# A two-layer kernel on one core: the skip connection moved from layer 1 into the row dispatch, and layer 1's operations placed anew

## The chip, the core and the metric

The kernel runs on one core of a Trainium2 chip. The core has five instruction streams: TensorE (PE, matrix products into PSUM), VectorE (DVE), ScalarE (ACT), GpSimd (POOL) and SyncE (SP, which here only issues DMAs). Each stream runs its instructions in the order of its own queue and waits on semaphores for the others. The metric is the device time of one execution in microseconds (us), lower is better.

## The reference

The input x is 32 images of 128 channels and 56x56 pixels, fp32. Two layers follow one another.

Layer 0 is a depthwise 7x7 convolution, a LayerNorm over channels, and a mixture of experts on the T = 100352 normalized rows of 128 channels: each row is routed to its two best of 8 experts, an expert takes 15680 rows at most in order of priority, and each row's result comes back scaled by its gate.

```
logits = xf @ Wg + bg
topv, topi = jax.lax.top_k(logits, K)            # K = 2
...
h = gelu(einsum('ecd,edf->ecf', eb, W1) + b1)
y = einsum('ecf,efd->ecd', h, W2) + b2
...
return input + x_skip + moe_out
```

So layer 0's output is a sum of three things: the image itself, the normalized rows, and what the experts add.

Layer 1 is a 1x1 convolution (cv1), a branch with a 3x3 depthwise convolution, and a branch with a Mamba block: LayerNorm, a projection to 256 channels and a gate z, a causal convolution over 4 positions, and a state space recurrence with 16 states per channel over the 3136 positions of an image:

```
def step(h, inp):
    dA_t, dBu_t, C_t = inp
    h = dA_t * h + dBu_t
    return (h, jnp.einsum('bds,bs->bd', h, C_t))
```

dA is exp(dt * A), dBu is dt * B * x. The two branches are joined by a second 1x1 convolution and added to the layer's input.

## The kernel before

**Layer 0.** The convolution runs first (to about 1500 us) and writes the normalized rows into `res_d` in DRAM. Within each image row of 56 pixels the rows lie in reversed order. Then the routing is worked out (to 1766 us): for each row two slots in `buf_d`, and two gates.

*Dispatch* (1773 to 3939 us) takes 14 columns of 112 rows at a time, 56 times. SP loads them from `res_d` into `xg0`; ScalarE copies them to `xg1` (line 854, 128x1792 values); VectorE writes a gate and a row number, taken from the table `backs`, behind each row in both (lines 856, 857); and GpSimd issues 14 indirect DMAs from each of the two, each of which scatters 128 rows of 130 words into `buf_d` (line 859), 1568 in all. The tiles `xg` have 6 buffers, so loads run ahead. A scatter waits for the completion of the one eight before it. Half way through, `weights` prepares layer 1's constants on several engines. This part of the kernel is ordered by an automatic scheduler.

*Experts* (3940 to 5881 us) load tiles of 128 rows from `buf_d`, transpose them, run the two matrix products with Gelu between, scale by the gate, and add the result into `res_d` at the rows' places by 984 indirect scatter-adds that GpSimd issues (line 911).

**Layer 1** (5883 us to the end) takes an image in NQ1 = 7 groups of CH1 = 448 positions, 224 groups in all, and in each group 16 *units*, one per state. The 256 channels lie as 128 partitions x 2 halves. What is done once in a group:
- `fetch` loads x1 (the image's 448 positions) and yg (four tiles of 112 rows of `res_d`).
- `moe_pe` puts both into one PSUM tile: x1 by a product with the identity (line 1026), and each tile of yg by a product with `perm`, a permutation that turns the rows back into their order (line 1028). `moe_act` copies the sum to x1.
- cv1, the LayerNorm's factor (`rstd_act`, three small VectorE steps `rstd_dve`, of which steps 0 and 1 work in `aside`, a corner of the PSUM buffer da0), the projections, and dt (`sp_...`); `du_pool` is dt times the input on GpSimd (line 1245).
- `dd_pe` begins the PSUM sum py; `yz_dve` multiplies the finished sum by the gate; `out_pe` and `out_act` end the group.

What is done for each unit:
- `bc_load`: SP loads B and C, broadcast over partitions, for a pair of units.
- `db_pool`: GpSimd's product of du and B for a pair of units (line 1336, 128x1792).
- `exp_act`: ScalarE's two exps, one per half, into the PSUM buffer `da[u % 2]` (line 1354), so units take turns in two buffers.
- `scan_dve`: VectorE's recurrence over both halves (line 1373), in place in da, or into a tile `hs`.
- `cmul`: the product with C, on VectorE from da or on GpSimd from hs (line 1397).
- `carry_act`: ScalarE copies the last state to the head of db for the next group.
- `sum_pe`: TensorE adds the product into py (line 1286).

`MODE` has a letter for each unit: D has scan and product on VectorE; P has the scan into hs and the product on GpSimd; Q is P with the scan in two halves; M (not used before) splits the unit, first half with the product on VectorE, second half on GpSimd.

The order is written out by hand. `PLAN` and `UNITS` give each operation a key, a due time in units; all operations of all groups are sorted by 16 times the group (plus the unit) plus the key, and issued in that order, which so becomes the order of every engine's queue.

Of the kernel before, what the change touches and what calls it, by code (L numbers as in the profile page):

```python
# [13 lines left out]
C = 128  # L14
RW = C + 2
HW = 56
# [26 lines left out]
MODE = 'DQDDQDPPDDDDPDDP'  # L43
PRODS = 6
PLAN = (
    (-41.157, "fetch"),
    (-34.382, "moe_pe"),
    (-32.986, "moe_act"),
    (-28.346, "cv1_pe", "p_cvc", "cv1c"),
    (-27.384, "sq_act"),  # L50
    (-26.393, "cv1_pe", "p_cv1", "cv1t"),
    (-25.274, "cv1_act"),
    (-23.306, "var_pe"),
    (-23.291, "rstd_act"),
    (-23.185, "edges_act"),
    (-20.935, "rstd_dve", 0),
    (-20.876, "rstd_dve", 1),
    (-19.458, "rstd_dve", 2),
    (-19.126, "bc_pe"),
    (-18.367, "te_dve"),  # L60
    (-18.165, "te_act"),
    (-17.77, "z_pe", 0),
    (-16.927, "z_copy", 0),
    (-15.982, "z_pe", 1),
    (-15.86, "xm_pe", 0),
    (-15.811, "xm_pe", 1),
    (-14.784, "z_copy", 1),
    (-14.441, "z_silu"),
    (-14.388, "xm_act", 0),
    (-14.349, "xm_act", 1),  # L70
    (-13.504, "tables"),
    (-13.487, "px_pe"),
    (-11.507, "px_act"),
    (-11.215, "dt_pe", 0),
    (-10.684, "dt_pe", 1),
    (-10.326, "sp_abs", 0),
    (-9.043, "sp_abs", 1),
    (-8.458, "sp_exp"),
    (-7.656, "sp_one"),
    (-6.228, "sp_w"),  # L80
    (-5.252, "sp_pe", ("w", "e", "m")),
    (-5.135, "sp_ln"),
    (-5.019, "sp_pe", ("u",)),
    (-4.678, "lt_pe", range(0, 9)),
    (-4.117, "sp_act", 0),
    (-3.918, "sp_act", 1),
    (-3.032, "lt_act", 0),
    (-3.001, "du_pool"),
    (-2.343, "lt_act", 1),
    (2.033, "lt_silu"),  # L90
    (3.656, "dd_pe"),
    (18.599, "yz_dve", 0),
    (18.857, "yz_dve", 1),
    (23.328, "out_pe"),
    (25.003, "out_act"),
# [3 lines left out]
        (-5.892, "bc_load", "bb"),  # L99
        (-3.501, "bc_load", "cb"),  # L100
        (-2.818, "db_pool"),
        (-0.991, "exp_act"),
        (-0.076, "scan_dve"),
        (0.16, "cmul", 0),
        (1.245, "carry_act"),
        (3.662, "sum_pe"),
    ),
    (
        (-2.505, "db_pool"),
        (-0.83, "exp_act"),  # L110
        (-0.619, "scan_dve"),
        (1.229, "cmul", 0),
        (3.088, "carry_act"),
        (9.441, "sum_pe"),
    ),
    (
        (-11.504, "bc_load", "bb"),
        (-2.533, "bc_load", "cb"),
        (-2.288, "db_pool"),
        (-0.633, "exp_act"),  # L120
        (-0.074, "scan_dve"),
        (0.16, "cmul", 0),
        (1.407, "carry_act"),
        (3.828, "sum_pe"),
    ),
    (
        (-3.007, "db_pool"),
        (-1.559, "exp_act"),
        (-0.609, "scan_dve"),
        (-0.338, "carry_act"),  # L130
        (0.16, "cmul", 0),
        (2.009, "sum_pe"),
    ),
    (
        (-4.093, "bc_load", "bb"),
        (-3.639, "db_pool"),
        (-0.666, "bc_load", "cb"),
        (-0.482, "exp_act"),
        (0.865, "scan_dve"),
        (1.06, "cmul", 0),  # L140
        (1.786, "sum_pe"),
        (2.033, "carry_act"),
    ),
    (
        (-4.025, "db_pool"),
        (-1.052, "exp_act"),
        (-0.068, "scan_dve"),
        (0.16, "cmul", 0),
        (1.263, "carry_act"),
        (3.791, "sum_pe"),  # L150
    ),
    (
        (-5.791, "bc_load", "bb"),
        (-4.743, "db_pool"),
        (-2.416, "bc_load", "cb"),
        (-0.463, "exp_act"),
        (0.538, "scan_dve"),
        (0.678, "cmul", 0),
        (1.758, "carry_act"),
        (4.239, "sum_pe"),  # L160
    ),
    (
        (-5.64, "db_pool"),
        (-0.299, "exp_act"),
        (-0.211, "scan_dve"),
        (1.06, "cmul", 0),
        (5.047, "sum_pe"),
        (5.187, "carry_act"),
    ),
    (  # L170
        (-7.178, "bc_load", "bb"),
        (-4.153, "db_pool"),
        (-3.514, "bc_load", "cb"),
        (-1.218, "exp_act"),
        (-0.956, "scan_dve"),
        (0.16, "cmul", 0),
        (0.466, "carry_act"),
        (0.815, "sum_pe"),
    ),
    (  # L180
        (-4.714, "db_pool"),
        (-1.825, "exp_act"),
        (-0.406, "scan_dve"),
        (0.16, "cmul", 0),
        (0.742, "carry_act"),
        (1.653, "sum_pe"),
    ),
    (
        (-8.23, "bc_load", "bb"),
        (-5.573, "bc_load", "cb"),  # L190
        (-4.053, "db_pool"),
        (-1.1, "exp_act"),
        (-0.6, "scan_dve"),
        (0.16, "cmul", 0),
        (0.996, "carry_act"),
        (1.077, "sum_pe"),
    ),
    (
        (-3.777, "db_pool"),
        (-0.685, "exp_act"),  # L200
        (-0.409, "scan_dve"),
        (0.16, "cmul", 0),
        (1.104, "sum_pe"),
        (1.278, "carry_act"),
    ),
# [39 lines left out]
def tile_kernel(tc: tile.TileContext, a: dict, out: bass.AP):  # L245
# [14 lines left out]
    with (  # L260
# [573 lines left out]
        with (  # L834
# [13 lines left out]
            for q in range(QB):  # L848
# [15 lines left out]
                if q == QB // 2:  # L864
                    w3 = weights(w3p, w3t, p3t)
# [600 lines left out]
```

## Time and profile before

| What | Value |
|---|---|
| Median of 14 runs | 15851.67 us (15842.47 to 15862.2) |
| Profiled execution | 15851.65 us, span 15849.9 us from first to last instruction |
| Dispatch, from first scatter to last | 1773.05 to 3939.4 us |
| Experts | 3940 to 5881 us |
| Layer 1 | 5883 to 15849.9 us |
| Scatters of dispatch | 1568, busy 1647.1 us |
| ScalarE copies of xg | 56, mean 1.688 us |
| db products of layer 1 | 1792 (8 a group), mean 3.685 us |
| Whole scans of layer 1 | 2240 in da, 896 in hs, mean 2.02 and 2.01 us |

How to read the profile's lines. A line of a group has the source line, the engine, the operation, output <- inputs with partitions x elements, the count; then the busy time in us and the mean of one in ns; then the idle time of the engine just ahead of these instructions and what ended it. "issue" is time in which the engine waited for nothing that the profile shows. A line of the timeline has the start, the duration, the instruction, and in brackets the idle time before. In the slices, the span is cut into 40 equal parts, and each digit is an engine's busy share in tenths. In the table by stretch, each row has the bounds and the length of the stretch and each engine's busy time with its count of instructions; PEclk is TensorE's granted clock as a share of its full speed. Neighbouring instructions of VectorE and GpSimd overlap a little in the records, so a row of back-to-back instructions is measured from start to start.

### The profile page before, as it was taken

The numbers are of one execution on the slowest core, as the hardware profiler recorded it, in microseconds if no ns is written. First come the engines' busy times: TensorE is split into PE (matmuls) and PEld (weight loads), VectorE is DVE, ScalarE is ACT, GpSimd is POOL, SyncE is SP. The second block draws the span as 40 slices with busy tenths as digits, with TensorE's granted clock in tenths as the row PEclk, the third lists the DMA queues.
The fourth block names the chain that finished last, engine by engine and source line by source line (L and its number), as shares of the span: only waits on it lengthen the run. The fifth ranks groups of instructions, "written<-read, shape, count | busy, mean of one in ns | idle before, by whom it ended". The sixth has DMA issues, their size and how long they took to land. (4 is left out here: it accounts for less than half of the span.)

```text
span 15849.9 us, 247520 instructions
## 1 busy us (share of the span) xinstructions
PE 12824.6 (81%) x92981; PEld 7167.3 (45%) x92981; DVE 11116.6 (70%) x11366; ACT 10499.5 (66%) x21038; POOL 13337.8 (84%) x6330
## 2 busy tenths in 40 slices
PE   7996200000999999999999999999999999999998
PEld 7996100000777764444444444444444444444444
DVE  2655400000111119999999999999999999999999
ACT  4564200000444448888888888888888888888888
POOL 2443477777888879999999999999999999999999
PEclk9997555555999999999999999999999999999999
DMA  8885422222555545555555555555555555555555
GB/s 262 233 239 175 170 72 71 71 71 64 69 71 71 71 65 184 184 184 185 185 184 184 184 185 184 182 185 184 183 183 185 184 184 185 184 184 184 184 183 171
DMA packets 1325280, 2520.85 MB, mean 159 GB/s; under 512 B 139352, under 2 KB 777136, under 8 KB 1316400
## 3 DMA queue, kind: packets, MB, share of 16 engines
q1 hardware_dynamic: 1127600, 2310.57, 46.8%
q0 software_dynamic: 196480, 194.45, 7.2%
q8 instruction: 732, 11.99, 0.3%
q14 instruction: 468, 3.83, 0.1%
HBM read 2129.06 MB, written 375.43 MB: 158 GB/s over the span
## 5 line engine op out<-in xcount | busy, mean ns | idle before, releaser
L1336 POOL TENSOR_TENSOR db<-du,bb 128x1792 f32<-128x1792 f32 x1792 | 6582.7, 3685 | 1.2 <-DMA bb<-bc_d 1.0
L1354 ACT ACTIVATE da<-dt,aneg 128x449 f32<-128x449 f32 x7168 | 4540.0, 637 | 374.7 <-DVE r L1095 112.9
L1373 DVE TENSOR_TENSOR_SCAN da<-da,db 128x898 f32<-128x898 f32 x2240 | 4522.3, 2019 | 0.6 <-issue 0.5
L1286 PE MATMUL py<-prod,ident 64*64 64x448 f32 x28672 | 3224.9, 547 | 124.2 <-DVE prod L1397 115.7
L1397 POOL TENSOR_TENSOR prod<-hs,cb 128x896 f32<-128x896 f32 x1344 | 2606.9, 1940 | 239.1 <-issue 151.9
L1397 DVE TENSOR_TENSOR prod<-da,cb 128x896 f32<-128x896 f32 x2240 | 2438.6, 1089 | 136.2 <-DMA cb<-bc_d 18.9
L859 POOL DMA_INDIRECT buf_d<-xg,slot x1568 | 1647.1, 1050 | 523.2 <-issue 519.0
L911 POOL DMA_INDIRECT res_d<-ys,xb x984 | 1592.0, 1618 | 349.9 <-issue 282.6
L951 PE MATMUL ept<-ident,xb 128*128 128x128 f32 (+1 forms) x984 | 189.0, 274 | 2078.1 <-DMA xb<-buf_d 2077.7
L1373 DVE TENSOR_TENSOR_SCAN hs<-da,db 128x898 f32<-128x898 f32 x896 | 1784.7, 2012 | 0.1
L1286 PEld LDWEIGHTS py<-prod,ident 64*64 64x64 f32 x28672 | 1008.7, 132 | 1561.9 <-issue 1045.7
L1126 PE MATMUL p_xm<-te,wk 128*128 128x448 f32 x3584 | 1395.5, 540 | 0.0
L903 DVE TENSOR_TENSOR ys<-py,b2t 128x512 f32<-128x512 f32 (+2 forms) x256 | 170.8, 670 | 1729.2 <-PE py L897 1466.9
L856 DVE COPY xg<-gate 128x14 f32<-128x14 f32 x112 | 20.4, 185 | 1884.3 <-DMA buf_d<-xg,slot 1846.8
L854 ACT COPY xg<-xg 128x1792 f32<-128x1792 f32 x56 | 94.5, 1688 | 1821.4 <-DMA buf_d<-xg,slot 1775.8
L951 PEld LDWEIGHTS ept<-ident,xb 128*128 128x128 f32 (+1 forms) x984 | 124.6, 143 | 2081.8 <-issue 2080.8
L897 PEld LDWEIGHTS py<-w2t,hh 128*128 128x128 f32 x7872 | 937.9, 191 | 191.6 <-issue 118.9
L897 PE MATMUL py<-w2t,hh 128*128 128x128 f32 x7872 | 987.4, 278 | 14.8 <-ACT hh L893 9.4
L1126 PEld LDWEIGHTS p_xm<-te,wk 128*128 128x128 f32 x3584 | 671.8, 189 | 665.7 <-issue 568.0
L379 PE MATMUL pc<-xc,toep 112*112 112x112 f32 (+1 forms) x8192 | 938.2, 270 | 40.1 <-ACT toep L368 36.3
L1258 PE MATMUL p_l<-xh,dwd 64*64 64x224 f32 x16128 | 907.3, 352 | 21.9 <-ACT dt L1240 1.8
L1377 DVE TENSOR_TENSOR_SCAN hs<-da,db 128x449 f32<-128x449 f32 x896 | 924.5, 1073 | 0.5 <-ACT da L1354 0.3
(241 smaller groups left out, 20283.2 us busy)
## 6 DMA issues: line engine op xcount, KB each, us to landing
bb<-bc_d SPq DMA_DIRECT2D x1792, 448.0 KB
cb<-bc_d SPq DMA_DIRECT2D x1792, 448.0 KB
toep<-toep_d SPq DMA_DIRECT2D x448, 392.0 KB
buf_d<-zero SPq DMA_DIRECT2D x28, 2275.0 KB
xb<-buf_d SPq DMA_DIRECT2D x240, 260.0 KB
xt<-in_x SPq DMA_DIRECT2D x32, 1568.0 KB
res_d<-xa SPq DMA_DIRECT2D x128, 392.0 KB
xg<-res_d SPq DMA_DIRECT2D x56, 896.0 KB
```

Source lines behind the costliest of these rows:

```text
L379: nc.tensor.matmul(pc[:, c, :, lo:hi], lhsT=tp[c // 2][:, c % 2, 6 - 2 * o : 8 - 2 * o, :], rhs=s4[:, c, :, lo + o - 1 : hi + o - 1], star ...
L859: apart(nc.gpsimd.indirect_dma_start(out=buf_d[:, :], out_offset=bass.IndirectOffsetOnAxis(ap=slots[k][:, o + j : o + j + 1], axis=0), in_ ...
L897: nc.tensor.matmul(py[:n, j, :], lhsT=hh[:, k, j * 128 : j * 128 + n], rhs=w2t[:, k, :], start=k == 0, stop=k == KF - 1,)
L911: apart(nc.gpsimd.indirect_dma_start(out=res_d[:, :], out_offset=bass.IndirectOffsetOnAxis(ap=xb[:n, j, C + 1 : C + 2].bitcast(I32), axis= ...
L1126: nc.tensor.matmul(p[:, :CH1], lhsT=s["wk"][:, k, hs], rhs=d["te"][:, k : k + CH1], start=k == 0, stop=k == DC - 1 and not first,)
L1258: nc.tensor.matmul(d["p_l"][r][k * HD : (k + 1) * HD, : CH1 // 2], lhsT=s["dwd"][rs, t, rs], rhs=d["xh"][rs, dy + k * R : dy + (k + 1) * R ...
L1286: nc.tensor.matmul(ps[r][h * HD : (h + 1) * HD, :CH1], lhsT=lhsT(rs, h), rhs=rhs[rs, h, :], start=start, stop=stop,)
L1336: nc.gpsimd.tensor_tensor(dbp[i // 2].rearrange("p k (h t) -> p k h t", h=2)[:, :, :, 1:], st[g]["du"].unsqueeze(1).to_broadcast(both), un ...
L1354: e = nc.scalar.activation(da[:, h * W1 : (h + 1) * W1], st[g]["dt"][:, h, :], AF.Exp, scale=s["aneg"][:, h, i : i + 1])
L1373: scans.append(nc.vector.tensor_tensor_scan(hs, da, dbs[i], 0.0, ALU.mult, ALU.add))
L1377: scans.append(nc.vector.tensor_tensor_scan(hs2[h][:, hh], da[:, hh], dbs[i][:, hh], 0.0, ALU.mult, ALU.add))
L1397: eng.tensor_tensor(w["prod"], w["hs"][0][:, :, 1:], w["cb"], ALU.mult)
```

## The change

The change has two parts.

**In layer 0's dispatch** a new function `skip` makes the sum of image and normalized rows for half an image at a time, 64 parts, and stores it into a new DRAM tensor `sum_d` in the rows' natural order. The experts now add into `sum_d`, so their row numbers `backs` are made in that order, too. Layer 1 reads only `sum_d`, and `moe_pe` only transposes. The copies of xg move from ScalarE to VectorE; `perm` is made in the dispatch rather than at the program's start; ScalarE copies the skip's sums out of PSUM and issues their stores.

```
-        mean_w = const.tile([128, 128], F32, name="mean_w")
+        mean_w = const.tile([128, 1], F32, name="mean_w")
...
-            nc.tensor.matmul(p[:, 0:1], lhsT=mean_w, rhs=cv1b, start=True, stop=True)
+            mean_c = wt.tile([128, C], F32, name="mean_c")
+            nc.vector.memset(mean_c, 1.0 / C)
+            nc.tensor.matmul(p[:, 0:1], lhsT=mean_c, rhs=cv1b, start=True, stop=True)
...
+            def skip(n, h):
+                t0 = (n * TPI + h * HT) * TT
+                xt = sk.tile([C, HT * TT], F32, name="xs")
+                nc.sync.dma_start(out=xt, in_=x_d[n, :, h * HT * TT : (h + 1) * HT * TT])
+                xr = sk.tile([TT, HT, C], F32, name="xr")
+                rows = [v[t0 : t0 + HT * TT, :].rearrange("(k p) c -> p k c", p=TT) for v in (res_d, sum_d)]
+                nc.sync.dma_start(out=xr, in_=rows[0])
+                for j0 in range(0, HT, 4):
+                    w = min(4, HT - j0)
+                    p = psk.tile([TT, 4, C], F32, name="p_sk")
+                    nc.tensor.matmul(p[:, :w], lhsT=perm, rhs=xr[:, j0 : j0 + w], start=True, stop=False)
+                    for j in range(w):
+                        nc.tensor.matmul(
+                            p[:, j, :], lhsT=xt[:, (j0 + j) * TT : (j0 + j + 1) * TT], rhs=ident,
+                            start=False, stop=j == w - 1,
+                        )
+                    nc.scalar.copy(xr[:, j0 : j0 + w], p[:, :w])
+                nc.scalar.dma_start(out=rows[1], in_=xr)
...
-                    nc.scalar.copy(xgs[1][:, :, :C], xgs[0][:, :, :C])
+                    nc.vector.tensor_copy(xgs[1][:, :, :C], xgs[0][:, :, :C])
...
+                    for _ in range(-(-len(parts) // (TT // XT * (QB - q) - p0 // XT))):
+                        skip(*parts.pop(0))
...
-                        out=res_d[:, :],
+                        out=sum_d[:, :],
```

HT is 14, so a part is 14 tiles of 112 rows. The tiles of `skip` have 2 buffers, its PSUM tiles 3.

**In layer 1** the modes and all keys are new, exp is issued by halves with a key each, hs has 3 buffers and x1 has 4 instead of 5. The lists of which operations touch different bytes (`near`, `free`, `decay`, where `halves` and `apart` stood) are kept in another way.

```
-MODE = 'DQDDQDPPDDDDPDDP'
+MODE = 'PPDDMDPPDDPDPDDD'
...
-    (-41.157, "fetch"),
-    (-34.382, "moe_pe"),
+    (-60.5589, "fetch"),
+    (-32.6293, "moe_pe"),
...
-    (-20.935, "rstd_dve", 0),
-    (-20.876, "rstd_dve", 1),
-    (-19.458, "rstd_dve", 2),
+    (-22.4112, "rstd_dve", 0),
+    (-22.4112, "rstd_dve", 1),
+    (-20.1575, "rstd_dve", 2),
...
-    (-4.117, "sp_act", 0),
-    (-3.918, "sp_act", 1),
-    (-3.001, "du_pool"),
+    (-3.7463, "sp_act", 0),
+    (-3.7368, "sp_act", 1),
+    (-1.8387, "du_pool"),
...
 UNITS, unit 4:
-        (-4.093, "bc_load", "bb"),
-        (-3.639, "db_pool"),
-        (-0.666, "bc_load", "cb"),
-        (-0.482, "exp_act"),
-        (0.865, "scan_dve"),
-        (1.06, "cmul", 0),
-        (1.786, "sum_pe"),
-        (2.033, "carry_act"),
+        (-7.6159, "bc_load", "bb"),
+        (-3.5327, "db_pool"),
+        (-3.253, "bc_load", "cb"),
+        (-0.0755, "exp_act", 0),
+        (0.2559, "exp_act", 1),
+        (0.491, "scan_dve", 0),
+        (0.705, "scan_dve", 1),
+        (0.9114, "cmul", 0),
+        (1.0371, "cmul", 1),
+        (1.0707, "carry_act"),
+        (3.718, "sum_pe"),
...
-            d["x1"] = three.tile([C, CH1], F32, name="x1", bufs=5)
-            nc.sync.dma_start(out=d["x1"], in_=x_d[n, :, q * CH1 : (q + 1) * CH1])
...
-            nc.tensor.matmul(p[:, :CH1], lhsT=ident, rhs=d["x1"], start=True, stop=False)
             for j in range(TPC1):
-                nc.tensor.matmul(
-                    p[:, j * TT : (j + 1) * TT], lhsT=yg[:, j, :], rhs=perm, start=False, stop=j == TPC1 - 1
-                )
+                nc.tensor.transpose(p[:, j * TT : (j + 1) * TT], yg[:, j, :], ident[:TT, :TT])
```

The order in which VectorE goes through a group is new with the keys. From unit 0 on it has: scans 0, 1, 2, 3, product 2, the two yz, product 3, the half scans of 4, half product 4, scan 5, product 5, scans 6, 7, 8, product 8, scan 9, rstd steps 0 and 1, product 9, scans 10, 11, rstd step 2, product 11, scans 12, 13, 14, product 13, te, product 14, scan 15, product 15. GpSimd makes the whole products of units 0, 1, 6, 7, 10 and 12 and half of unit 4.

## The prediction

> **What bounds the kernel now.** I read the page first, then the busy time by stage, then the groups of the steady part of layer 1, then the order of single instructions on VectorE and GpSimd, and last the row scatters of the dispatch. The page, engines and slices:
>
> ```profile
> PE 12824.6 (81%) x92981; PEld 7167.3 (45%) x92981; DVE 11116.6 (70%) x11366; ACT 10499.5 (66%) x21038; POOL 13337.8 (84%) x6330
> DVE  2655400000111119999999999999999999999999
> POOL 2443477777888879999999999999999999999999
> ```
>
> No engine leads by much, and the shares mix stages. From the sixteenth slice on (5883 us, layer 1) VectorE and GpSimd are full; in slices 5 to 9 (dispatch) VectorE is nearly idle and GpSimd issues scatters. The busy time by stage, one stretch inside the dispatch and one inside layer 1:
>
> ```profile
> core 0: us, PE busy (x) PEld busy (x) DVE busy (x) ACT busy (x) POOL busy (x), PEclk, DMA share, GB/s
> 2450.00:4600.00 2150.00, 641.18 (x3632) 462.19 (x3633) 133.54 (x306) 332.43 (x450) 1659.61 (x1388) 0.65 0.32 69
> 7000.00:15500.00 8500.00, 8137.87 (x60065) 3817.92 (x60064) 8375.80 (x6537) 7392.12 (x15322) 8166.82 (x2940) 1.00 0.58 184
> ```
>
> In layer 1 VectorE is busy 98.5%, GpSimd 96.1%, TensorE 95.7%: VectorE bounds it, the two others stand close behind. The groups of that stretch:
>
> ```profile
> L1336 POOL TENSOR_TENSOR db<-du,bb 128x1792 f32<-128x1792 f32 x1538 | 5649.5, 3685 | 1.0 <-DMA bb<-bc_d 1.0
> L1397 POOL TENSOR_TENSOR prod<-hs,cb 128x896 f32<-128x896 f32 x1154 | 2238.3, 1940 | 198.9 <-issue 125.2 <-DMA cb<-bc_d 29.4 <-DVE r L1095 27.8
> L1397 DVE TENSOR_TENSOR prod<-da,cb 128x896 f32<-128x896 f32 x1922 | 2092.4, 1089 | 117.4 <-DMA cb<-bc_d 18.3 <-PE p_var L1073 1.6 <-issue 1.3
> L1245 POOL TENSOR_TENSOR du<-dt,xm 128x896 f32<-128x896 f32 x192 | 371.7, 1936 | 133.3 <-ACT dt L1240 129.9 <-DMA cb<-bc_d 2.9
> L1354 ACT ACTIVATE da<-dt,aneg 128x449 f32<-128x449 f32 x6150 | 3895.1, 637 | 315.6 <-DVE r L1095 97.8 <-DVE prod L1397 80.1 <-DVE hs L1377 4.8
> L1028 PE MATMUL p_moe<-perm,yg 112*128 112x112 f32 x1536 | 200.2, 273 | 0.0
> L1026 PE MATMUL p_moe<-x,ident 128*128 128x448 f32 x384 | 195.6, 591 | 0.0
> ```
>
> 1538 db products at 8 per group are 192.25 groups: 8500/192.25 = 44.2 us per group, 224 groups in all. GpSimd is busy 8166.82/192.25 = 42.5 us of each and waits 0.69 for dt and 1.03 ahead of products; TensorE is busy 42.3. On VectorE the distance from start to start matters, because neighbours overlap:
>
> ```profile
> 10017.17 3.93 DVE L1373 TENSOR_TENSOR_SCAN hs<-da,db 128x898 f32<-128x898 f32 x2
> 10021.03 2.01 DVE L1373 TENSOR_TENSOR_SCAN da<-da,db 128x898 f32<-128x898 f32 x1
> 10023.13 1.09 DVE L1397 TENSOR_TENSOR prod<-da,cb 128x896 f32<-128x896 f32 x1
> 10024.13 2.03 DVE L1373 TENSOR_TENSOR_SCAN da<-da,db 128x898 f32<-128x898 f32 x1
> ```
>
> A scan followed by another scan takes 1.93 (two in 3.86), a product 1.00 to 1.01, and a scan followed by its own product 2.10 to 2.13: about 0.12 to 0.17 is spent on the result that the next instruction reads.
>
> **Layer 1, VectorE.** Before, per group: 14 whole scans x 1.94, 2 pairs of half scans x 1.98, 10 products x 1.01, 7 of them directly behind their scan (+0.12), and 2.03 of yz, te and rstd: 27.16 + 3.96 + 10.10 + 0.84 + 2.03 = 44.09, against 44.2 measured. After: 15 whole scans, one pair (unit 4, mode M), 9 products and a half (0.52), and by the new order only 3 directly behind their scan: 29.10 + 1.98 + 9.09 + 0.52 + 0.36 + 2.03 = 43.08. So 1.01 us less work per group.
>
> **Layer 1, GpSimd.** It keeps 8 db, 6 whole products and du, and gains half a product: 0.97 (half of 1.94) to 1.07 (with some fixed part). 42.5 + 1.0 = 43.5 becomes its floor. The wait for dt goes (du_pool is queued some 5 us behind sp_act), and most of the product waits with it. GpSimd is thus slower than VectorE's bare 43.08: the group cannot fall below 43.5.
>
> **Layer 1, waits that the new order adds.** A scan needs both exps of its unit, 0.64 us each, and an exp can only overwrite its da buffer when the scan and VectorE product of two units before, or rstd's use of da0, are done. In the new order rstd steps 0 and 1 stand ahead of product 9 and then scan 10: exp 10 starts when rstd 1 has left da0, only product 9 (1.01) covers its two halves (1.28 plus a hand-over), so scan 10 waits about 0.45. rstd step 2 waits likewise for the second exp of unit 12, about 0.2; and the exps of unit 4 queue on ScalarE behind silu and its table loads, about 0.2. Behind a waiting scan the whole of VectorE waits, and through it GpSimd's next product and TensorE's sum. 43.08 + 0.85 = 43.95. Bounds: no wait at all but GpSimd's floor, 43.5; twice these waits, 44.8. I take 43.95, since every wait counted comes from durations in these rows. GpSimd's loop through the last product of a group (unit 12), the next group's db and its scans is about 12.9 (a product and three db) + 30 (scans 2 to 12) + waits, 43.7, so it adds nothing. The second half product follows its scan through one more hs buffer (3 for 2), which frees VectorE from GpSimd's lag.
>
> **Layer 1, TensorE, ScalarE, DMA.** Four products with perm (200.2/192.25 = 1.04 us) and one with ident (1.02) become four transposes; a product has two records and the experts' transposes have one each, so 4 x 0.13 = 0.52 (1.04 if two). TensorE falls from 42.3 to about 41; I cost this at nothing because VectorE is later, and without that cover it would be a gain. ScalarE loses nothing but order: same 32 exps, 16 carries plus one. The x1 load goes: 448 columns per group, hidden before and hidden after. The new bookkeeping (near, free, decay) issues no instruction; mean_c adds one memset to the weights' preparation, under the scatters. Together: (43.95 - 44.2) x 224 = -56 us. Its prologue and tail differ by a few instructions, +-5, taken as 0.
>
> **Dispatch.** 1568 scatters stand on GpSimd, the stage's bound, while all that is added goes to other engines. Where the scatters stand in time, counted alone:
>
> ```profile
> core 0: us, POOL busy (x), PEclk, DMA share, GB/s
> 1773.00:2043.00 270.00, 205.68 (x212) 0.50 0.33 94
> 2100.00:3700.00 1600.00, 1213.63 (x1143) 0.50 0.24 72
> ```
>
> 1.27 us each in the first stretch and 1.40 after, though the first holds the denser row loads: loads do not set the pace. The 64 skip parts add 128 loads of 0.8 MB on SP and 64 stores on ScalarE's queue. Each scatter waits for the one eight before it, about 10 us of slack, and a landing is late by 2 to 3 us in a load burst, so I take 0 for them; the other bound prices every burst as the present ones look at worst, 1.3 us x 192 = 250 us. On TensorE, at the half clock of these rows, a part is 14 small products and 4 of 512 columns, about 15 us, two parts per 36 to 39 us of scatters: hidden, as are ScalarE's copies back. SP's row loads xg now queue between the skip's loads, but are three steps ahead. The stores into sum_d end before the experts' first scatter-add.
>
> The copy of the rows (56 x 128x1792) moves from ScalarE (1.69 us each) to VectorE: off the scatters' engine either way. Its cost to GpSimd is not in the trace. The nearest rows by the timeline are seven VectorE writes of 128x128 (1.46 us together) and the scatter issued beside them, which keeps its 0.97; and, among the experts, a scatter-add beside a two-input VectorE product of 0.69 us, which takes 1.84 instead of its neighbours' 1.55:
>
> ```profile
> 1827.95 1.46 DVE L750 TENSOR_SCALAR dwd<-ident,dw 128x128 f32<-128x128 f32 x7
> ```
> ```profile
> 1827.95 0.97 POOL L859 DMA_INDIRECT buf_d<-xg,slot  x1 [0.30 <-issue]
> ...
> 5834.41 1.84 POOL L911 DMA_INDIRECT res_d<-ys,xb  x1 [0.30 <-issue]
> ```
>
> The second row gives +0.29 us per two-input product, or 0.42 of its length: 0.3 to 0.8 us per copy, 16 to 45 us. The ends are nothing and the copy's whole length, at most 2 us (one element a cycle, as 128x896 products take 1.01): 56 x 2 = 115. The dwd row is nearest, a write with a single input like the copy, so I take 0 for the copies and +10 for the stage as a whole: the start (the first copy and two affine_selects, about 2 us, now ahead of scatters) and some 8 for a few scatters held.
>
> A rule against this: the Trainium skill, page "SBUF — State Buffer", section "SBUF: two separate sides", says that a two-port VectorE operation, which an fp32 SBUF copy is, locks GpSimd out of the port pair that it writes DMA descriptors through. By it, at 2 elements a cycle, each copy would hold a scatter for about 1 us, an estimate of +56 to +62 in place of +10. The dwd row shows no such hold beside the scatters, but no copy of this size stands beside one here.
>
> **Sum.** 15851.65 (profiled run; span 15849.9 plus 1.75; the median of the 14 runs is 15851.67, so no correction) - 56 + 10 = 15805.
>
> **Rivals.**
> - GpSimd's floor is reached: the waits fall beside GpSimd's, 43.5 per group, (43.5 - 44.2) x 224 = -157, 15690 to 15770. For it: the order leaves slack on every GpSimd product; against it: VectorE was never stalled before, and now is by exp.
> - Dispatch is slower: VectorE's copies hold scatters (20 to 115) or the 192 extra bursts stretch them (up to 250). It decides from +56 on, 1 us per copy or 0.3 us per burst; 15850 to 16000. For it: the L911 row; against it: the dwd row and the unchanged pace in the stretches.
> - Layer 1 gains nothing: exp waits of 1.1 instead of 0.85 or late TensorE sums hold 44.2 to 44.6, 0 to +90: 15840 to 15930. For it: ScalarE is at 87% in the steady part and its order is new; against it: each wait that I could count is priced.
> - The change does what it says on the instruction lists, so that rival has no place.
>
> **How the numbers follow.** What a measurement of this kernel can tell from no change is about 0.2%, 32 us. Forecast (15770 to 15835) 0.40; GpSimd floor 0.17; slower dispatch 0.23; no gain in layer 1 0.20. Faster by over 32 us (below 15820): 0.17 + 0.34 of the forecast + 0.03 of a dispatch loss on a better layer 1 = 0.54; within: 0.06 + 0.05 + 0.06 = 0.17; slower: 0.29. The range 15690 to 15920 leaves out the worst dispatch (0.12) and a layer 1 better than GpSimd's floor or worse than 44.6 (0.06).
>
> **What would show it.** Layer 1 right: db products 43.95 us x 1/8 apart, VectorE idle about 0.8 per group in front of scan 10, r and unit 4's scans; wrong if idle stands ahead of GpSimd's db or of TensorE's sums. Dispatch right: scatters at 1.27 to 1.40; wrong if single scatters of 2 to 3 us stand beside the VectorE copies, or the wait before scatters grows in load bursts, or the last stretch waits for xg. A layer 1 period under 43.5 would overthrow the GpSimd count.

## The result, and the profile after

The changed kernel takes 16045.48 us (median of 6 runs, 16037.81 to 16061.19), the kernel before 15852.11 us (median of 28 beside it): ratio 1.0123, 95% interval 1.0113 to 1.0133. It is 193 us slower, where 46 us faster was forecast. Its profiled execution took 16036.08 us, its span is 16034.2 us, 184.3 more than before. By the starts of GpSimd's instructions the spans divide so:

| Stage | before, us | after, us | difference |
|---|---|---|---|
| to the first scatter | 1773.0 | 1779.6 | +6.6 |
| dispatch, first to last scatter | 2165.2 | 2378.5 | +213.3 |
| to the first scatter-add of the experts | 37.0 | 37.7 | +0.7 |
| experts, first to last scatter-add | 1904.5 | 1902.8 | -1.7 |
| to the first db of layer 1 | 49.2 | 45.1 | -4.1 |
| layer 1, first to last db | 9892.6 | 9864.5 | -28.1 |
| the rest | 28.3 | 25.9 | -2.4 |

Layer 1 gained 28 us, and the dispatch lost 213. The page of the changed kernel, engines, GpSimd's slices and the group of the scatters (busy time, mean ns | idle time ahead of them):

```profile
PE 13324.9 (83%) x93941; PEld 7429.7 (46%) x93941; DVE 11044.0 (69%) x11199; ACT 10489.1 (65%) x21430; POOL 13434.4 (84%) x6554
POOL 2443465657788888999999999999999999999999
L899 POOL DMA_INDIRECT buf_d<-xg,slot x1568 | 1547.0, 987 | 835.1 <-issue 510.7
```

In four slices of the dispatch GpSimd is down from 7 to 5 or 6. Each scatter is shorter than before (987 ns against 1050), but GpSimd idles 835 us ahead of them instead of 523. What for is in its waits, first those of the kernel before, from 1770 to 3945 us, then those of the changed kernel and of its SP and ScalarE, from 1770 to 4200 us (us in total, times, longest):

```profile
POOL buf_d L859 <- DMA xg<-res_d: 4.0, 1, 4.0
```
```profile
POOL buf_d L899 <- issue: 510.7, 1545, 19.8
POOL buf_d L899 <- DMA xg<-res_d: 315.0, 17, 26.7
```
```profile
SPq L870 <- remote: 992.2, 26, 90.3
SPq L873 <- DMA sum_d<-xr: 252.9, 39, 11.1
```
```profile
ACT xr L883 <- remote: 1134.1, 83, 28.3
ACT xr L883 <- issue: 334.3, 36, 29.0
ACT xr L883 <- PE p_sk L879: 310.7, 106, 14.2
```

Before, GpSimd waited 4.0 us for xg; now it waits 315 us, 17 times. Not all of that is lost, because between the pauses it issues a scatter every 1.26 us instead of 1.38 on average. SP issues the loads of xg in one queue with the skip's loads, and the skip's load of the image (line 870) stood there for 992 us, up to 90 us at once. It waits for a buffer that TensorE has to read. And ScalarE's copies (line 883), which wait for nothing but TensorE's products, waited 1134 us for something that the profile can't name. The order of time, first on ScalarE:

```profile
1932.29 0.37 ACT L883 COPY xr<-p_sk 112x256 f32<-112x256 f32 x1 [16.21 <-remote]
1960.29 0.58 ACT L883 COPY xr<-p_sk 112x512 f32<-112x512 f32 x1 [27.63 <-remote]
1988.29 0.58 ACT L883 COPY xr<-p_sk 112x512 f32<-112x512 f32 x1 [27.42 <-remote]
2016.29 0.58 ACT L883 COPY xr<-p_sk 112x512 f32<-112x512 f32 x1 [27.41 <-remote]
2033.09 0.37 ACT L883 COPY xr<-p_sk 112x256 f32<-112x256 f32 x1 [16.21 <-remote]
```

The distances are 28.00, 28.00, 28.00 and 16.80 us, as from a clock. A copy of 512 columns needs a group of 10 TensorE matmul records, 2 for perm and 8 for the identity, each with its weight load: 20 instructions. A copy of 256 columns needs 6 records, 12 instructions. Both come to 1.40 us per instruction. TensorE's own records don't show it: a group some 600 us later stands there as done at once, its copy much later, and GpSimd's pause follows:

```profile
2601.20 1.02 PE L877 MATMUL p_sk<-xr,perm 112*112 112x512 f32 x2
2602.06 1.04 PE L879 MATMUL p_sk<-ident,xs 128*112 128x128 f32 x8
```
```profile
2625.12 0.58 ACT L883 COPY xr<-p_sk 112x512 f32<-112x512 f32 x1 [14.81 <-remote]
2651.72 0.58 ACT L883 COPY xr<-p_sk 112x512 f32<-112x512 f32 x1 [26.01 <-remote]
```
```profile
2613.78 0.32 SPq L873 DMA_DIRECT2D xr<-res_d  x1
2661.52 0.33 SPq L870 DMA_DIRECT2D xs<-in_x  x1
2669.32 0.32 SPq L873 DMA_DIRECT2D xr<-res_d  x1
2669.95 1.36 SPq L893 DMA_DIRECT2D xg<-res_d  x1
```
```profile
2654.76 0.96 POOL L899 DMA_INDIRECT buf_d<-xg,slot  x1 [0.30 <-issue]
2681.60 1.27 POOL L899 DMA_INDIRECT buf_d<-xg,slot  x1 [25.88 <-DMA xg<-res_d]
```

The group recorded as ended at 2603.10 lets its copy go at 2625.12, 22 us later. (The profile says of itself that ends of matmuls are modelled; the copy's start is not.) SP stands from 2614 to 2661 for the image's buffer, issues xg at 2669.95, and GpSimd, out of rows since 2655.72, goes on at 2681.60. In these pauses of GpSimd TensorE catches up. Let a group's time run from the copy before it, or from its own first record on TensorE if that is later, to its own copy. Of the 56 groups of 4 tiles that fall whole into pauses of over 3 us, 54 took under 4 us. The skip's 256 groups took more than 4 us in 98 cases, 1430 us together, nearly all while scatters were being issued.

In layer 1, the same stretch of 8500 us as before, and VectorE's and GpSimd's waits in it:

```profile
7000.00:15500.00 8500.00, 8075.33 (x59125) 3703.33 (x59126) 8294.07 (x6363) 7370.25 (x15536) 8363.40 (x3141) 1.00 0.58 179
```
```profile
DVE hs L1416 <- ACT da L1400: 75.6, 194, 0.5
DVE da L1416 <- ACT da L1400: 43.9, 165, 0.4
DVE yz L1332 <- PE py L1342: 15.2, 28, 0.5
```
```profile
POOL du L1301 <- DVE prod L1429: 87.5, 157, 1.1
POOL prod L1429 <- issue: 11.5, 30, 0.5
```

1542 db products are 192.75 groups of 44.1 us; from first db to last it is 9864.5/223.875 = 44.06 us per group against 44.19 before. VectorE is busy 8294.07/192.75 = 43.03 us of it (predicted 43.08), GpSimd 43.39 (predicted 43.5), and VectorE waits 119.5/192.75 = 0.62 us for exp.

### The profile page after: what moved, and what is told of

Read it like the earlier page. It is cut to its first block, busy times and chain, and to the rows that moved or that the text cites. A ratio compares the mean times of both kernels' runs of the same rounds, so it can differ in the third digit from the quotient of the medians.

```text
span 16034.2 us, 248818 instructions
## 1 busy us (share of the span) xinstructions
PE 13324.9 (83%) x93941; PEld 7429.7 (46%) x93941; DVE 11044.0 (69%) x11199; ACT 10489.1 (65%) x21430; POOL 13434.4 (84%) x6554
## 5 line engine op out<-in xcount | busy, mean ns | idle before, releaser
L1416 DVE TENSOR_TENSOR_SCAN da<-da,db 128x898 f32<-128x898 f32 (+1 forms) x2240 | 4273.4, 1926 | 55.0 <-ACT da L1400 52.7
L1416 DVE TENSOR_TENSOR_SCAN hs<-da,db 128x898 f32<-128x898 f32 (+1 forms) x1568 | 2913.2, 1881 | 110.9 <-ACT da L1400 88.0
L899 POOL DMA_INDIRECT buf_d<-xg,slot x1568 | 1547.0, 987 | 835.1 <-issue 510.7
L1429 DVE TENSOR_TENSOR prod<-da,cb 128x896 f32<-128x896 f32 x2016 | 2183.3, 1083 | 44.7 <-DMA cb<-bc_d 5.0
L953 POOL DMA_INDIRECT sum_d<-ys,xb x984 | 1589.8, 1616 | 351.0 <-issue 285.9
L877 PE MATMUL p_sk<-xr,perm 112*112 112x512 f32 (+1 forms) x512 | 349.2, 774 | 1217.3 <-issue 761.2
L883 ACT COPY xr<-p_sk 112x512 f32<-112x512 f32 (+1 forms) x256 | 133.9, 533 | 1789.4 <-remote 1134.1
L995 ACT COPY xc<-ept 128x512 f32<-128x512 f32 (+1 forms) x248 | 143.9, 580 | 1349.9 <-issue 621.5
L383 PEld LDWEIGHTS pc<-xc,toep 112*112 112x112 f32 x8192 | 884.1, 185 | 47.3 <-ACT toep L372 41.1
L413 POOL TENSOR_TENSOR xa<-xa,lng 112x896 f32<-112x896 f32 x128 | 267.1, 2087 | 749.4 <-ACT xa L410 688.2
```

The costliest lines, as they stand in the source:

```text
L383: nc.tensor.matmul(pc[:, c, :, lo:hi], lhsT=tp[c // 2][:, c % 2, 6 - 2 * o : 8 - 2 * o, :], rhs=s4[:, c, :, lo + o - 1 : hi + o - 1], star ...
L413: nc.gpsimd.tensor_tensor(xa, xa, lng.unsqueeze(1).to_broadcast([TT, w, C]), ALU.mult)
L877: nc.tensor.matmul(p[:, :w], lhsT=perm, rhs=xr[:, j0 : j0 + w], start=True, stop=False)
L899: apart(nc.gpsimd.indirect_dma_start(out=buf_d[:, :], out_offset=bass.IndirectOffsetOnAxis(ap=slots[k][:, o + j : o + j + 1], axis=0), in_ ...
L953: apart(nc.gpsimd.indirect_dma_start(out=sum_d[:, :], out_offset=bass.IndirectOffsetOnAxis(ap=xb[:n, j, C + 1 : C + 2].bitcast(I32), axis= ...
L1416: scan = nc.vector.tensor_tensor_scan(w["hs"][h][:, hh], da[:, hh], dbs[i][:, hh], 0.0, ALU.mult, ALU.add)
```

## Experiments

**What holds the dispatch.** The first theory to go was the one that the prediction had as its rival, the copy on VectorE. Alone in the kernel before:

```
-                    nc.scalar.copy(xgs[1][:, :, :C], xgs[0][:, :, :C])
+                    nc.vector.tensor_copy(xgs[1][:, :, :C], xgs[0][:, :, :C])
```

> The kernel before with one line changed: the copy of the rows from xg0 to xg1 is on VectorE. In the changed kernel the scatters that follow a copy run at 1.26 us where those of before lost some 3 us per step of 28 (172 us in all). If the copy's engine is the reason, dispatch falls from 2165 to about 2060 us and the time from 15852 to about 15745. If the reason lies in the skip's other traffic, nothing changes (15840 to 15862). If VectorE's copy holds GpSimd for its length (1.1 us x 56), the time is about 15910.

15847.81 us against 15849.77, ratio 1.000 (0.999 to 1.001); dispatch 2166.9 us. Neither a gain nor a loss. The scatters beside the copies do get longer, which fits the hold that the Trainium skill's page "SBUF — State Buffer" (section "SBUF: two separate sides") describes, though mostly by less than the copy's 1.1 us. Timeline of this run, GpSimd and VectorE:

```profile
2609.31 1.66 POOL L859 DMA_INDIRECT buf_d<-xg,slot  x1 [0.30 <-issue]
2611.28 1.10 POOL L859 DMA_INDIRECT buf_d<-xg,slot  x1 [0.30 <-issue]
```
```profile
2609.28 1.15 DVE L854 COPY xg<-xg 128x1792 f32<-128x1792 f32 x1 [18.21 <-DMA buf_d<-xg,slot]
```

The scatter beside this copy takes 1.66 us instead of 0.96. One row is not enough, since single scatters of 1.8 us stand in the kernel before, too; but over all 56 copies the longest scatter beside each has a median of 1.33 us (1.18 to 2.42), against 0.97 beside ScalarE's copies in the kernel before. It costs nothing, because GpSimd is not what the stage waits for: it issues at 1.27 us, but 1568 scatters take 2165 us, 1.38 each, in this run, in the kernel before and in the runs below that are neither starved nor slowed. Over its last 120 scatters, with no loads left, the kernel before issues one every 1.400 us. So they go away at about 1.40 us each, and a short hold of GpSimd is made up. TensorE's 1.40 us per instruction is the same number; whether that is more than a coincidence no run shows.

Then the skip without its products, with half of them, and with the other half (here and below the times of kernels that leave something out, of the slowed ones and of those without a ratio are those of single runs):

```
 skip_no_pe: only loads and store
-                for j0 in range(0, HT, 4):
...
-                    nc.scalar.copy(xr[:, j0 : j0 + w], p[:, :w])
                 nc.scalar.dma_start(out=rows[1], in_=xr)
 skip_perm_only: no products with the identity
-                    for j in range(w):
-                        nc.tensor.matmul(
-                            p[:, j, :], lhsT=xt[:, (j0 + j) * TT : (j0 + j + 1) * TT], rhs=ident,
...
 skip_ident_only: no products with perm
-                    nc.tensor.matmul(p[:, :w], lhsT=perm, rhs=xr[:, j0 : j0 + w], start=True, stop=False)
```

> The changed kernel without the skip's products and copies: the loads of image and rows stay, and the rows are stored as they came, so image and reordering are left out of the sum. Theory A, late TensorE: with no products the buffers come free at once, SP is not held, the waits of GpSimd for xg (315 us) go, dispatch falls from 2379 to 2060 to 2100 us and the time to 15720 to 15770. Theory B, the 128 loads and 64 stores themselves hold SP or the DMA engines: the waits stay, dispatch stays above 2300 us, the time above 15960.

> The changed kernel without the 14 products with the identity per part (the image is left out); the 4 products with perm of up to 512 columns stay: 16 TensorE instructions per part instead of 72, half of the columns. Theory A1, each TensorE instruction takes 1.4 us while scatters flow: 22 us per part, 1.5 parts per step of 35 us, so it just keeps up: waits for xg under 50 us, dispatch 2080 to 2130 us, time 15740 to 15800. Theory A2, lateness goes by columns: about 50 us per part, waits about half, dispatch about 2230 us, time about 15900. Theory B: as the full skip, over 2300 us.

> The changed kernel without the 4 products with perm per part (the normalized rows are left out of the sum); the 14 products with the identity stay: 56 TensorE instructions per part, half of the columns. Theory A1 (per instruction): 78 us per part against 24 us that are there, so waits for xg stay near those of the full skip, dispatch 2300 to 2370 us, time 15960 to 16040. Theory A2 (by columns): the same as with perm alone, dispatch about 2230 us, time about 15900.

| Run | time, us | dispatch, us | waits for xg, us | a 4-tile group, held |
|---|---|---|---|---|
| changed kernel | 16045 | 2378.5 | 315.0 | 28.0 us, 20 instructions |
| skip_no_pe | 15816.54 | 2165.5 | 2.6 | none |
| skip_perm_only | 15808.06 | 2166.3 | 2.5 | 5.6 us, 4 instructions |
| skip_ident_only | 16002.33 | 2342.1 | 275.3 | 22.4 us, 16 instructions |

The loads and the stores cost nothing (theory B falls). Two runs with the same number of columns on TensorE differ by 176 us of dispatch, as their instructions do: 1.40 us each, 5.6, 22.4 and 28.0 us per group. A1 stands, A2 falls. (The dispatch of a held kernel is not steady: the changed kernel's was 2378.5 and 2392.0 us in two profiles, so the 36 us between it and skip_ident_only are not read.) In all of these runs a weight load comes with each product, so 1.40 us per instruction can't be told from 2.80 us per pair. Dispatch without starvation came out at 2165, not at the 2060 to 2130 that I had expected, since the drain of 1.38 was not yet understood. ScalarE's copies with perm alone, then with the identity alone:

```profile
2106.21 0.59 ACT L878 COPY xr<-p_sk 112x512 f32<-112x512 f32 x1 [3.62 <-PE p_sk L877]
2112.52 0.37 ACT L878 COPY xr<-p_sk 112x256 f32<-112x256 f32 x1 [5.72 <-remote]
2118.81 0.59 ACT L878 COPY xr<-p_sk 112x512 f32<-112x512 f32 x1 [5.92 <-remote]
```
```profile
1973.74 0.58 ACT L882 COPY xr<-p_sk 112x512 f32<-112x512 f32 x1 [19.72 <-remote]
1996.14 0.58 ACT L882 COPY xr<-p_sk 112x512 f32<-112x512 f32 x1 [21.82 <-issue]
2007.34 0.37 ACT L882 COPY xr<-p_sk 112x256 f32<-112x256 f32 x1 [10.62 <-issue]
```

With perm alone half of them stand 4.9 to 6.3 us apart (median 5.6, with 512 columns as with 256) in place of 28, and 22 us per part fit into the scatters' time. With the identity alone the distances shown are 22.40 us for 16 instructions and 11.20 us for 8.

**Is it the scatters that hold TensorE?** The changed kernel, with GpSimd slowed by a useless write behind each scatter, of 768, 192 and 320 columns (the last two stand under `if parts:`, which holds in all 56 steps, so each run makes 1568 writes):

```
+            idle = dc.tile([128, 768], F32, name="idle")
...
                                 in_=xg[:, j, :], in_offset=None,
                             ), "scatter")
+                            nc.gpsimd.memset(idle, 0.0)
```

> The changed kernel with a write of 128x768 zeros by GpSimd behind every scatter, so that scatters are issued every 2.0 to 2.3 us instead of 1.26. Theory S1: TensorE is held only while scatters are issued faster than they drain (1.38 us each): a part's groups end within 2 to 4 us, GpSimd never waits for xg, and dispatch is 1568 times the pace, 3150 to 3600 us. Theory S2: TensorE gets one instruction per scatter, whatever the pace: 72 x 2.2 = 158 us per part, waits for xg of several hundred us on top.

> The changed kernel with a write of 128x192 zeros by GpSimd (about 0.26 us) behind every scatter: pace 1.40 instead of 1.26 us. Theory S1, TensorE is held only while scatters are issued faster than about one per 1.38 us: more work on GpSimd makes the stage shorter, no waits for xg, dispatch 2195 to 2220 us, time 15860 to 15890. Theory S4, TensorE is held at any pace near this one and free only near 1.9: waits for xg remain, dispatch 2350 us or more, time 16015 or more.

> The same with 128x320 zeros (about 0.37 us): pace 1.51 us. Theory S1: no waits for xg, dispatch 1568 x 1.51 = 2365 us, time about 16030, that is longer than with 192. Theory S4: some waits remain, dispatch above 2420 us.

| Run | pace of a scatter, median, us | 4-tile group, median, us | groups of over 4 us, together | waits for xg | dispatch, us | time, us |
|---|---|---|---|---|---|---|
| changed kernel | 1.263 | 3.5 (a quarter over 9.9) | 98, 1430 us | 315.0 | 2378.5 | 16045 |
| skip_paced_192 | 1.402 | 3.58 (a quarter over 4.3) | 59, 295 us | none | 2243.0 | 15878.83 |
| skip_paced_320 | 1.509 | 1.74 | none | none | 2405.3 | 16043.42 |
| skip_slow_scatter | 1.886 | 1.74 | none | none | 2992.9 | 16641.25 |

ScalarE's copies at the pace of 1.51 us:

```profile
2112.75 0.58 ACT L884 COPY xr<-p_sk 112x512 f32<-112x512 f32 x1 [1.73 <-issue]
2114.49 0.58 ACT L884 COPY xr<-p_sk 112x512 f32<-112x512 f32 x1 [1.15 <-issue]
```

With 0.14 us more of work per scatter the kernel is 167 us faster than the changed kernel, though still no faster than the kernel before (15860.77 us beside it). At 1.40 us the median group is as long as in the changed kernel, but the long ones go: one takes over 10 us instead of 58; at 1.51 and 1.89 no group takes over 4 us. So the hold comes with scatters issued faster than they drain (S1); S2 and S4 fall. By which path a backlog of scatters makes TensorE's results late no run here shows, nor whether its instructions themselves are late or only the signal of their end.

SP's order was a suspect, too: the skip's loads issued by ScalarE instead, so that SP has xg alone.

```
-                nc.sync.dma_start(out=xt, in_=x_d[n, :, h * HT * TT : (h + 1) * HT * TT])
+                nc.scalar.dma_start(out=xt, in_=x_d[n, :, h * HT * TT : (h + 1) * HT * TT])
...
-                nc.sync.dma_start(out=xr, in_=rows[0])
+                nc.scalar.dma_start(out=xr, in_=rows[0])
```

> The changed kernel with the skip's loads issued by ScalarE, so that SP has nothing but xg and is never held. Theory A: GpSimd no longer waits for xg, scatters take 2165 us, but then TensorE never gets the pauses in which it caught up: about 2165/100 = 22 parts are done by the end of the scatters, the other 42 follow at full speed (8 to 12 us each) ahead of the experts, 350 to 500 us: time 16150 to 16300, slower than the changed kernel. Theory B2, SP's order alone is the loss: dispatch 2165 and all parts done with it, time 15800 to 15830.

16027.8 us, dispatch 2378.1, waits for xg 345.3: neither. The waits of SP in this run:

```profile
SPq L893 <- DMA sum_d<-xr: 552.8, 9, 94.8
SPq L893 <- DMA xr<-res_d: 455.9, 6, 175.1
```

SP now waits with xg itself, for transfers that ScalarE issued and that share no bytes with it. By the program's waits they share a semaphore: the DMAs of both queues take turns in a set of eight, and a load waits for the transfer that used the same one before. A queue of its own did not part xg from the skip, and so what the pauses are worth to TensorE stayed untested by this run.

**Layer 1.** The new plan alone on the dispatch of before, then with one edit to its waits, then the same edit on the changed kernel:

```
 plan_only: MODE, PLAN, UNITS and the bookkeeping of after; no skip; moe_pe and x1's load as before
 plan_aside and after_aside add:
-            return free(i, (b, h), [(b, 1 - h)] if h < 2 else [])
+            return free(i, (b, h), ([(b, 1 - h)] if h < 2 else []) + (["aside"] if (b, h) == (0, 1) else []))
...
-                nc.vector.tensor_tensor(aside, aside, d.pop("v"), ALU.mult)
+                free(nc.vector.tensor_tensor(aside, aside, d.pop("v"), ALU.mult), "aside", [(0, 1)])
```

and likewise for rstd's other instructions on `aside`.

> The kernel before with the new modes, keys and bookkeeping of layer 1 alone: no skip, the rows added into the same tensor as before, ScalarE's copies, layer 1 loads the image and makes its 5 products in moe_pe as before (fetch at key -39 and 4 buffers for x1, for room). Theory P1: VectorE's chain with its exp waits sets the group, and TensorE's 1.5 us more are covered: 44.06 us per group as in the changed kernel, dispatch 2165, time 15815 to 15830. Theory P2: the lighter moe_pe is what the new order needs: 44.3 us and more, time 15870 and more.

> As the run with the new plan alone, but exps of the second half into da0 no longer wait for rstd's steps, which work in a corner of the first half's bank. Theory P1: scan 10 waits 0.39 us per group because its two exps start only behind rstd step 1; with one of them earlier product 9 covers the other, the wait goes, and the group falls to GpSimd's 43.4 plus small waits, 43.6 to 43.8: 60 to 100 us less, time 15720 to 15765. Theory P3: ScalarE's order lets another wait take its place: 44.0, time 15810 to 15825.

> The changed kernel with the one edit that took scan 10's wait away in the run with the new plan: exps of the second half into da0 don't wait for rstd's steps. Theory P1: on the light moe_pe the group falls from 44.06 by 0.4 to 0.55 us to 43.5 to 43.65, GpSimd's floor; time 15920 to 15955. Theory P4: with scan 10 earlier the wait for the last products of py (0.72 us in the run with the new plan) comes up here too: 43.9, time about 16010.

| Run | us per group | wait ahead of scan 10 | wait ahead of yz | time, us |
|---|---|---|---|---|
| before | 44.19 | 0 | 0 | 15852 |
| changed kernel | 44.06 | 0.39 | 0.08 | 16045 |
| plan_only | 44.46 | 0.39 | 0.73 | 15908.01, ratio 1.0036 (1.0023 to 1.0049) |
| plan_aside | 43.90 | 0 | 0.72 | 15785.91, ratio 0.9958 (0.9944 to 0.9972) |
| after_aside | 43.53 | 0 | 0.07 | 15907.23 |

VectorE's waits in the same stretch, plan_only, then plan_aside, then after_aside:

```profile
DVE yz L1308 <- PE py L1318: 138.7, 191, 1.3
DVE hs L1392 <- ACT da L1376: 75.3, 193, 0.5
```
```profile
DVE yz L1308 <- PE py L1318: 140.0, 194, 1.3
DVE hs L1392 <- ACT da L1376: 0.9, 2, 0.5
```
```profile
DVE da L1416 <- ACT da L1400: 43.1, 163, 0.3
DVE yz L1332 <- PE py L1342: 13.9, 26, 0.6
```

Two waits can be taken away one by one. The line `hs <- ACT da` is scan 10's: it goes with the edit and nothing takes its place (P1; P3 and P4 fall); the group falls by 0.55 us, more than the wait in the records: start to start scan 10 comes 0.47 us earlier, and r another 0.08. The line `yz <- PE py` is 0.72 us per group that goes with the lighter moe_pe: with the five products of before the new plan is slower than the old one (P2). (That run also loads the image again and fetches later, at key -39; the wait is for TensorE's sum, so TensorE's work is the likely cause, but the three were not parted.) With both gone the group is 43.53 us, GpSimd's own work: it is busy 8467.61 of 8500 us there, 99.6%.

**Both edits together.** The pace of 192 columns for the first 34 of 56 steps, and `aside`.

> The changed kernel with both edits that the runs point to: the write of 128x192 zeros behind each scatter of the first 34 of 56 steps (TensorE was done with the skip after 29 steps in the run paced by 192), and exps of the second half into da0 that don't wait for rstd's steps. If the two gains add: dispatch about 2200 us (180 less than in the changed kernel) and 43.53 us per group (138 less in all): 16045 - 180 - 138 = 15727, range 15705 to 15755, faster than before and than the new plan with that edit alone (15786). If TensorE is not done by step 34 and is held again, waits for xg come back: 15780 and more.

> The paced version with the exp edit once more, timed beside the kernel before on the chip of this comparison. If that chip drains a scatter in 1.38 to 1.40 us (before 15840 to 15865): 15705 to 15755, 0.7 to 0.9% faster than before. If it drains it in 1.27 us (before about 15660): 15666 as in the last run, no difference.

> The kernel before, for its profile on this chip. The mean distance of its scatters tells the chip's drain: 1.38 us with a time of 15850, or 1.27 us with a time of 15660; layer 1 is the same, 44.19 us per group.

> The changed kernel, for its profile on this chip. Theory S1: at a drain of 1.38 to 1.40 us TensorE is held as before (groups of 28.0 us, waits for xg of about 315 us), time 16045. At a drain of 1.27 us it is held little or not at all: dispatch about 2000 us, waits for xg under 50 us, time 15630 to 15680. If it is held at 1.27 us, too, the hold is not the chip's drain: waits over 200 us, time above 15850.

> The changed kernel with the exp edit on this chip: 138 us below the changed kernel on any chip, since layer 1 doesn't depend on the scatters: 15907 at a drain of 1.40 us, about 15500 to 15540 at 1.27 us.

The first comparison gave 15665.82 us beside 15662.66 for the kernel before, ratio 1.0004 (0.9994 to 1.0013). That chip ran the kernel before 189 us faster than all others did, and the scatters that have no write behind them took 1.27 us each there, 1.262 over the last 120, where those of the second chip took 1.400. The second, on a chip like the others: 15715.05 us (15689.37 to 15737.55) beside 15853.77, ratio 0.9907 (0.9891 to 0.9924), 0.9% faster than before; its dispatch took 2196.7 us and its groups 43.52, so the two gains add as expected. There the profiles gave, for the kernel before, 1.381 us per scatter and 44.18 per group; for the changed kernel 16056.74 us, dispatch 2392.0, waits for xg 344.1 and groups of 28.0 us again; with the exp edit 15874.54 us, 182 less than the changed kernel where 138 were expected: layer 1 gave 125, and the held dispatch happened to be 52 shorter (2340.2). The scatters of the paced version, the first stretch with the write and the second without, on the first chip and then on the second:

```profile
2000.00:2600.00 600.00, 412.00 (x420) 0.70 0.70 209
3300.00:3900.00 600.00, 456.05 (x473) 0.50 0.24 73
```
```profile
2000.00:2600.00 600.00, 413.82 (x421) 0.71 0.72 210
3300.00:3900.00 600.00, 458.29 (x440) 0.50 0.23 69
```

With the write both issue 420 scatters in 600 us; without it the first chip 473, the second 440. At the same pace of 1.40 a 4-tile group of TensorE took 1.74 us (median) on the first chip and 2.9 on the second: it is held where scatters drain more slowly, by one run on each. Whether the changed kernel without the pace would be held on the first chip was not seen, as no later run fell on such a chip.

## Why the prediction was wrong

- **TensorE in the dispatch: the step that failed.** "On TensorE, at the half clock of these rows, a part is 14 small products and 4 of 512 columns, about 15 us, two parts per 36 to 39 us of scatters: hidden." Durations from stretches without scatters were carried into one with them. A held part is 28.0 x 3 + 16.8 = 100.8 us, and it was not hidden: its buffers came free too late for SP, SP's xg too late for GpSimd, and the dispatch took 213 us more. Unheld, as at the pace of 1.51 us, a part takes some 6 us (3 x 1.74 + 0.87), so the 15 us were ample there. The row that could have warned stood in the trace of before: the products into p_wo (four records), recorded as ended at 1866.12 us, let ScalarE's copy of them go at 1870.24 only, beside the scatters, with the same unnamed releaser:

```profile
1864.89 1.23 PE L817 MATMUL p_wo<-cvgt,wop 128*128 128x128 f32 x4
```
```profile
1870.24 0.37 ACT L821 COPY wo<-p_wo 128x256 f32<-128x256 f32 x1 [4.97 <-remote]
```

- **SP's queue.** "SP's row loads xg now queue between the skip's loads, but are three steps ahead." Three steps are some 110 us; SP stood for one buffer up to 90 us at once and 992 us in all. This follows from the first.
- **Dispatch is bound by GpSimd.** Half right: GpSimd starved is what counts, but unstarved it is the drain of the scatters, 1.38 to 1.40 us, that sets 2165 us. The prediction had the 1.40 beside the 1.27, said rightly that loads don't set it, and left it unexplained.
- **The copy on VectorE** was taken at 0 and costs 0 (ratio 1.000); by the rule weighed against it, +56 to +62. The scatter beside it is lengthened, in the median from 0.97 to 1.33 us, but not the stage. Of the +10 for the stage as a whole nothing shows: the +6.6 ahead of the first scatter is no more than two profiles of the kernel before differ by (1773.0 and 1779.7).
- **The rival "dispatch is slower"** had the right place and sign, with the wrong causes: copies 0, bursts 0 (skip_no_pe at 2165.5).
- **Layer 1** gained 28 us instead of 56: 44.06 per group, not 43.95. VectorE's busy time was right within 0.05 us (43.03 against 43.08). Of the waits, taken start to start against the runs that don't have them, scan 10's was right (0.47 against 0.45), r's smaller (0.08 against 0.2) and that of unit 4's first half scan larger (0.29 against 0.2). Not counted were 0.23 for unit 4's pair of half scans, 2.21 instead of 1.98, and 0.08 at yz.
- **TensorE in layer 1** was "at nothing because VectorE is later". Going by plan_only, the lighter moe_pe is worth 0.40 us per group (44.46 against 44.06), some 88 us: without it the new plan loses 56 us to the old one.
- **GpSimd's floor of 43.5** was right: 43.53 once scan 10's wait is gone.
- **The sum without the failed step.** With no products at all (skip_no_pe) the kernel takes 15816.54 us, near the 15805 forecast. That nearness is partly luck: layer 1 gained half of what was counted on, and the dispatch cost nothing instead of 10 us.

## What to carry to other kernels

An engine that is idle in a stage is not free there: before work is moved beside a stream of GpSimd's indirect DMAs, look at how late that engine's results arrive in that stage, by the start of what waits for them, not by its own recorded ends. Work that other loads queue behind (here SP's loads behind a buffer that TensorE frees) turns such lateness into starvation of the engine that bounds the stage. And a new order's waits are best priced one by one: of the two that mattered here, one (0.39 us per group) was a dependence on bytes that nobody shared.

## What the runs showed of the hardware that was not expected

- While scatters of 128 rows of 520 bytes are issued every 1.26 us and drain at 1.40, TensorE's results come at the rate of one weight load and product per 2.80 us, whatever their columns: 5.6, 16.8, 22.4 and 28.0 us for 4, 12, 16 and 20 instructions. At a pace of 1.51 us it does not. The Trainium skill's page "SBUF — State Buffer" says in its section "Who interferes with whom", of the engines' ports into SBUF, that TensorE never waits on anyone; TensorE's results do come late here, but as the path is open no run shows whether it is on those ports.
- The rate at which scatters go away differs from chip to chip: 1.40 us each where the kernel before takes 15852 us, 1.27 or less on the one chip where it takes 15663. The difference of the two drains over 1568 scatters, (1.381 - 1.262) x 1568 = 187 us, is an estimate that fits the 189 us; the kernel before was not profiled on that chip.
- More work on the engine that bounds a stage made the stage shorter: 0.14 us per scatter on GpSimd took 135 us off the changed kernel's dispatch.
